# Edge stages of a graph kernel: a hand-fixed order, group by group, in place of the scheduler's

## The chip, the cores and the metric

The kernel runs on one core of a Trainium2 chip. The metric is the device time of one execution in microseconds; beside it stands one profiled execution, whose span and instructions the profile page and the trace show.

## What is computed

Four layers act on x (3125 nodes of 256 numbers), with 53125 edges (src, dst, type, weight). Two of them are graph layers, and the change touches only these:

```python
# heads' graph layer (4 heads of 64), on LayerNorm(x)
feats = einsum('nd,hdo->hno', x, Ws) + bs
score = a_s[:, src] + a_d[:, dst] + aw_e * elem + ab
w = exp(-relu(score / 20))
out = segment_sum(w * feats[:, dst], src) / segment_sum(w, src)
# relations' graph layer (200 relations), on LayerNorm(x)
score = h[src] @ w_src + h[dst] @ w_dst + rel_e @ w_rel
alpha = exp(leaky_relu(score)); alpha = alpha / alpha
agg = segment_sum((h[src] + rel_emb[etype]) @ weight_neighbor * alpha, dst)
node = relu(agg) + where(in_deg > 0, h @ loop_weight, h @ evolve_loop_weight)
```

Each layer's result is added to x. Behind the heads' layer comes a layer of 16 experts with the two best per node, behind the relations' layer a feed-forward layer for half of the nodes ("depths").

## The kernel before

The kernel runs in one program: it sorts the edges by node for the heads (from 0 to about 430 us), computes the table of features, does the heads' edges (430 to 1172), the experts together with the moves of the second sort (to about 1720), the relations' features (to about 1872), the relations' edges (to about 2560) and the depths (to the end).

**Tiles and groups.** The sort has put the edges into tiles of 128, ordered by node tile (128 nodes). There are 25 node tiles, 24 with 18 edge tiles and the last with 8, so 440 edge tiles. `edge_groups` (L714) cuts each node tile into groups of 6, 74 in all; the first of a node tile is called head, the last one last.

**An edge stage.** `edge_stages` (L724) makes three functions, used by the heads' and the relations' edges alike:

- `gather` (L749): at a head, `spread` (L744) loads the row numbers of the whole node tile, broadcast to all partitions (`wide`, 576 KB, two buffers), through SP's queue. Then GpSimd (POOL) issues six indirect gathers (L754) of feature rows into `rows` (three buffers). VectorE (DVE) makes `oh`, the one-hot of each edge's node (L762, three buffers), and `hot`, a one-hot from `wide` (L771): one per group for the heads, three for the relations.
- `message` (L775): TensorE (PE) multiplies `hot` by the nodes' own values into `ps_near` (L780); DVE reduces it (`near`, L787). Then `messages` follows. For the heads (L916) these are three short operations on `s` (L919 to L921), two exponentials on ScalarE (ACT, L924 and L925) and the product `msg` on DVE (L926). For the relations (L1308) they are the weight (L1310 and L1279 to L1282, with an exponential on ACT at L1280), a one-hot of the relation written into the free columns of `rows` (L1313), and six scalings of `oh` to `ohw` on ACT (L1319); `rows` is itself the message.
- `add` (L793): PE sums the messages of a node tile in `ps_sums` (L798). At the last group, SP loads `more` (L804), DVE adds it (`acc`, L806), and `finish` follows. For the heads (L933) it divides, adds to x and calls `done` (L966), which after every five node tiles (and the last two and three) does the next layer norm (`norm_tiles`, L152: statistics, a square root on ACT at L160, scaling), stores its rows, and transposes them and computes the experts' logits on PE. For the relations (L1324) it transposes counts (`ps_cnt`, L1330, copied by ACT at L1333), multiplies them by the relations' features (`ps_rel`, L1336), multiplies the nodes by two loop weights (`ps_loop`, L1343) and adds all to x on DVE (`agg` L1349, `has` L1352 and L1353, `x` L1350 and L1355).

**What sets the order.** `pipelined` (L811) writes step s as gather of group s, message of s-1, add of s-2, and before them one step of `fill`. For the heads, `fill` is the ranking of the second sort, on DVE: after its loads (L224) and one-hots with four matmul steps on PE (L383), 25 steps of five operations over 128 x 416 (such as L441 and L444); for the relations there is none. The Tile framework's scheduler then chooses each engine's order of instructions itself, by readiness and priority; it may run an instruction of a later step ahead of one of an earlier step. Engines wait for each other by semaphores, and a buffer of a pool is handed out again when its last reader is done.

Of the kernel before, what the change touches and what calls it, by code (L numbers as in the profile page):

```python
# [9 lines left out]
F32 = mybir.dt.float32  # L10
BF16 = mybir.dt.bfloat16
# [3 lines left out]
OP = mybir.AluOpType  # L15
# [3 lines left out]
P = 128  # L19
# [3 lines left out]
class _Kernel:  # L23
# [697 lines left out]
                out.append((b, self.first[b] + j, m, j == 0, j + m == n))  # L721
        return out

    def edge_stages(self, pool, st, table, width, into, near, others, messages, W, sums, finish):  # L724

        nc, G = self.nc, self.GRP
        nv = near.shape[3]  # L730
        now = {}


        hold, sums2 = self.ps_a("ps_hold"), self.ps_a("ps_sums")
        numbers = hold[:, :256]
        nc.vector.tensor_copy(numbers, self.iota[:, :256])
        self.numbers, self.weights_ps = numbers, hold[:, 512:]

        def spread(i, b):

            t = pool.tile([P, self.tiles[0] // 2, 2 * P + 8], BF16, name=f"wide{i}")
            src = st["wide"][i][self.first[b] : self.first[b] + self.tiles[b], :]
            src = src.rearrange("(o k i) p -> o k (i p)", o=1, i=2)
            nc.sync.dma_start(  # L744
                t[:, : self.tiles[b] // 2, : 2 * P], src.to_broadcast([P, self.tiles[b] // 2, 2 * P])
            )
            return t

        def gather(g, b, k, n, head, last):  # L749
            if head:  # L750
                now[b] = [spread(i, b) for i in range(len(st["wide"]))]
            rows = pool.tile([P, G, into], F32, name="rows", bufs=3)
            for j in range(n):
                nc.gpsimd.indirect_dma_start(  # L754
                    out=rows[:, j, :width], out_offset=None, in_=table,
                    in_offset=bass.IndirectOffsetOnAxis(
                        ap=st["idx"][:, k + j : k + j + 1], axis=0
                    ),
                )
            sh = [P, n, P]  # L760
            oh = pool.tile([P, G, P], F32, name="oh", bufs=3)
            nc.vector.tensor_tensor(  # L762
                oh[:, :n, :], numbers[:, None, :P].to_broadcast(sh),
                st["row"][:, k : k + n, None].to_broadcast(sh), op=OP.is_equal,
            )
            lo = (k - self.first[b]) // 2
            hots = []
            for i, (at, _) in enumerate([(self.pcol1, None)] + others):
                w = now[b][min(i, 1)][:, lo : lo + n // 2, : 2 * P]
                t = pool.tile([P, G // 2, 2 * P], BF16, name=f"hot{i}", bufs=2)  # L770
                nc.vector.tensor_scalar(t[:, : n // 2, :], w, at, None, op0=OP.is_equal)  # L771
                hots.append(t)
            return rows, oh, hots

        def message(g, b, k, n, head, last, rows, oh, hots):  # L775
            pe = self.ps_b("ps_near")
            picks = [near[:, b]] + [v for _, v in others]
            for j in range(n):
                for i, (t, v) in enumerate(zip(hots, picks)):
                    nc.tensor.matmul(  # L780
                        pe[:, j * 3 * nv : (j + 1) * 3 * nv],
                        t[:, j // 2, j % 2 * P : (j % 2 + 1) * P],
                        v.rearrange("p q v -> p (q v)"),
                        start=(i == 0), stop=(i == len(picks) - 1),
                    )
            own = pool.tile([P, G, nv], F32, name="near")
            nc.vector.tensor_reduce(  # L787
                own[:, :n, :],
                pe[:, : n * 3 * nv].rearrange("p (j q v) -> p j v q", q=3, v=nv), AX.X, OP.add,
            )  # L790
            return messages(k, n, rows, own, oh)

        def add(g, b, k, n, head, last, oh, msg):  # L793
            if head:
                now["sum"] = sums2[:, b % 2 * 512 : (b % 2 + 1) * 512]
            ps = now["sum"]
            for j in range(n):
                nc.tensor.matmul(  # L798
                    ps[:, :W], oh[:, j, :], msg[:, j, :],
                    start=(head and j == 0), stop=(last and j == n - 1),  # L800
                )
            if last:
                more = pool.tile([P, W], F32, name="more")
                nc.sync.dma_start(more, sums[b])  # L804
                acc = pool.tile([P, W], F32, name="acc")
                nc.vector.tensor_add(acc, ps[:, :W], more)  # L806
                finish(b, acc)

        return gather, message, add

    def pipelined(self, stages, fill=()):  # L811


        groups, done = self.edge_groups(), {}
        fill = iter(fill)
        for step in range(len(groups) + len(stages) - 1):
            if step > 2:
                next(fill, None)
            for i, stage in enumerate(stages):
                g = step - i  # L820
                if 0 <= g < len(groups):
                    done[g] = stage(g, *groups[g], *(done.pop(g, None) or ()))
        for _ in fill:
            pass

# [53 lines left out]
    def heads_edges(self, st, fill, done):  # L881
# [26 lines left out]
        with self.tc.tile_pool(name="edge0", bufs=2) as pool:  # L908
            near = pool.tile([P, NT, 3, H], BF16, name="near0p", bufs=1)
            tmp = pool.tile([P, NT, H], F32, name="near0t", bufs=1)  # L910
            self.parts([near[:, :, q, :] for q in range(3)], self.near0[:, :NT, :], tmp)

            own = pool.tile([P, MT, H], F32, name="own", bufs=1)
            own_part(own, st["val"], lambda t, h: t[:, :, h])

            def messages(k, n, rows, near, oh):  # L916
                s = pool.tile([P, G, H], F32, name="s0")
                s = s[:, :n, :]
                nc.vector.tensor_add(s, near[:, :n, :], rows[:, :n, HO:])  # L919
                nc.vector.tensor_add(s, s, own[:, k : k + n, :])  # L920
                nc.vector.tensor_scalar(s, s, -1.0 / 20.0, 0.0, op0=OP.mult, op1=OP.min)  # L921
                msg = pool.tile([P, G, W], F32, name="msg0", bufs=3)
                w = self.weights_ps[:, : n * H].rearrange("p (j h) -> p j h", h=H)
                nc.scalar.activation(w, s, AF.Exp)  # L924
                nc.scalar.activation(msg[:, :n, HO:], s, AF.Exp)  # L925
                nc.vector.tensor_tensor(  # L926
                    msg[:, :n, :HO].rearrange("p j (h o) -> p j h o", o=O),
                    rows[:, :n, :HO].rearrange("p j (h o) -> p j h o", o=O),
                    w[:, :, :, None].to_broadcast([P, n, H, O]), op=OP.mult,
                )  # L930
                return oh, msg

            def finish(b, acc):  # L933
                if b == NT - 1:
                    nc.vector.tensor_scalar(acc[:, HO:], acc[:, HO:], self.norow, None, op0=OP.add)
                r = pool.tile([P, H], F32, name="r0")
                nc.vector.reciprocal(r, acc[:, HO:])
                v = acc[:, :HO].rearrange("p (h o) -> p h o", o=O)
                nc.vector.tensor_tensor(v, v, r[:, :, None].to_broadcast([P, H, O]), op=OP.mult)
                nc.vector.tensor_add(self.x[:, b, :], self.x[:, b, :], acc[:, :HO])  # L940
                done(b)

            self.pipelined(self.edge_stages(
                pool, st, self.table0, W, W, near, [], messages, W, self.sums0, finish
            ), fill)

# [323 lines left out]
    def relations_edges(self, st):  # L1272
# [27 lines left out]
        with self.tc.tile_pool(name="edge1", bufs=2) as pool:  # L1300
# [4 lines left out]
            for i, w in enumerate(("L1_gnn_loop_weight", "L1_gnn_evolve_loop_weight")):  # L1305
                nc.sync.dma_start(lw[:, :, i, :], a[w].rearrange("(c p) d -> p c d", p=P))

            def messages(k, n, rows, near, oh):  # L1308
                s = pool.tile([P, 3, G], F32, name="s1")
                nc.vector.tensor_add(s[:, 0, :n], near[:, :n, 0], rows[:, :n, D])  # L1310
                weight(s[:, 1, :n], s[:, 0, :n], s[:, 2, :n])
                sh = [P, n, R]
                nc.vector.tensor_tensor(  # L1313
                    rows[:, :n, R0:], self.numbers[:, None, :R].to_broadcast(sh),
                    st["val"][:, k : k + n, None].to_broadcast(sh), op=OP.is_equal,
                )
                ow = pool.tile([P, G, P], F32, name="ohw", bufs=3)
                for j in range(n):
                    nc.scalar.activation(  # L1319
# [4 lines left out]
            def finish(t, acc):  # L1324
# [33 lines left out]
                    )  # L1358

            others = [(self.pcols[:, 1 + i : 2 + i], self.rel_p[:, i]) for i in range(-(-R // P))]  # L1360
            self.pipelined(self.edge_stages(
                pool, st, self.table1, R0, W, near, others, messages, W, self.sums1, finish
            ))

# [191 lines left out]
```

## Time and profile before

| what | value |
|---|---|
| median of 3 runs | 2857.28 us (2856.35 to 2861.86) |
| the profiled execution, its own time | 2845.15 us |
| its span | 2842.8 us |
| mean granted clock of PE | 0.822 of full |
| first and last gather of an edge stage (L754) | 429.7 and 2544.1 us |
| gathers: times, median of one | 880, 946 ns |

The span is what the profile's instructions cover; the profiled execution's own time lies 2.35 us over it, and the median of the runs 12 us over that. An instruction group gives its busy time, the mean of one, and how long its engine was idle just before, with the releaser: what that idle time ended on. "remote" is a semaphore event for which the profile has no instruction that ended then. The chain of waits follows the work that ended last back from releaser to releaser; "another core or an unknown queue" is the same unknown there.

### The profile page before, as it was taken

The numbers are of one execution on the slowest core, as the hardware profiler recorded it, in microseconds if no ns is written. First come the engines' busy times: TensorE is split into PE (matmuls) and PEld (weight loads), VectorE is DVE, ScalarE is ACT, GpSimd is POOL, SyncE is SP. The second block draws the span as 40 slices with busy tenths as digits, with TensorE's granted clock in tenths as the row PEclk, the third lists the DMA queues.
The fourth block names the chain that finished last, engine by engine and source line by source line (L and its number), as shares of the span: only waits on it lengthen the run. The fifth ranks groups of instructions, "written<-read, shape, count | busy, mean of one in ns | idle before, by whom it ended". The sixth has DMA issues, their size and how long they took to land.

```text
span 2842.8 us, 24381 instructions
## 1 busy us (share of the span) xinstructions
PE 1878.6 (66%) x7534; PEld 1126.4 (40%) x7534; DVE 1446.3 (51%) x3397; ACT 390.7 (14%) x1097; POOL 1167.4 (41%) x1198
## 2 busy tenths in 40 slices
PE   3169554854544443399999991447878778785298
PEld 0024232543433332356666660323434334343166
DVE  4876225476665343644422224445655556549721
ACT  0000010010000000100112120112222222221012
POOL 4235306576654646034411115036666666650000
PEclk9999996676666667577799996768889888898599
DMA  2000325343444433144499982254545455431000
GB/s 83 0 3 5 104 89 137 93 130 112 115 100 114 116 100 101 49 150 130 131 316 318 317 291 84 87 156 131 148 129 148 130 142 149 128 85 34 8 21 18
DMA packets 258938, 334.04 MB, mean 118 GB/s; under 512 B 30861, under 2 KB 192407, under 8 KB 258807
## 3 DMA queue, kind: packets, MB, share of 16 engines
q1 hardware_dynamic: 197527, 191.26, 21.3%
q0 software_dynamic: 51920, 132.68, 17.6%
q10 hardware_dynamic: 9360, 8.52, 0.9%
q8 instruction: 61, 1.00, 0.1%
q14 instruction: 70, 0.57, 0.1%
HBM read 298.38 MB, written 33.98 MB: 117 GB/s over the span
## 4 chain that ended last, share of the span: by engine, by line
PE 39%; DVE 14%; issue 10%; POOL 9%; another core or an unknown queue 8%; DMA 4%; ACT 1%; SPq 0%; DVEq 0%; POOLq 0%; ACTq 0%
PE ps_sums L798 10%; PE ps_h L1130 9%; POOL rows L754 9%; PE ps_y L1147 4%; PE s_mv L560 3%; DVE cmp L1426 3%; PE ps_hid L1453 3%; PE ps_out L1464 3%; DMA rows<-table,s_idx 3%; DVE msg L926 2%; DVE hot L771 2%; PE ps_x_t L173 1%; PE ps_h_t L173 1%; PE ps_f L1264 1%
## 5 line engine op out<-in xcount | busy, mean ns | idle before, releaser
L754 POOL DMA_INDIRECT rows<-table,s_idx x880 | 848.6, 964 | 725.0 <-issue 240.4
L798 PE MATMUL ps_sums<-msg,oh 128*128 128x260 f32 x880 | 306.6, 519 | 261.8 <-DVE msg L926 143.1
L798 PE MATMUL ps_sums<-rows,ohw 128*128 128x457 f32 x880 | 414.0, 616 | 62.8 <-ACT ohw L1319 54.1
L798 PEld LDWEIGHTS ps_sums<-msg,oh 128*128 128x128 f32 x880 | 226.6, 265 | 325.1 <-issue 250.1
L560 PE MATMUL s_mv<-s_hv,s_hp 128*128 128x200 f16 (+1 forms) x832 | 246.8, 472 | 89.9 <-DVE s_hv L555 89.9
L798 PEld LDWEIGHTS ps_sums<-rows,ohw 128*128 128x128 f32 x880 | 179.0, 215 | 217.5 <-issue 149.6
L1130 PE MATMUL ps_h<-w,x_t 128*128 128x512 f32 x520 | 256.1, 638 | 0.0
L771 DVE TENSOR_SCALAR hot<-wide,pcols 128x768 bf16<-128x768 bf16 (+1 forms) x296 | 175.4, 597 | 73.9 <-PE ps_near L780 63.0
L560 PEld LDWEIGHTS <-s_hp 128*128 128x128 f16 x832 | 122.1, 147 | 208.7 <-issue 180.3
L762 DVE TENSOR_TENSOR oh<-ps_hold,s_row 128x768 f32<-128x768 f32 (+1 forms) x148 | 139.9, 946 | 125.7 <-remote 73.5
L1119 POOL DMA_INDIRECT xg<-xtab,who x65 | 61.9, 952 | 345.1 <-PE ps_x_t L173 302.6
L569 POOL DMA_INDIRECT s_tab<-s_rec,s_to x130 | 147.8, 1137 | 115.1 <-ACT s_rec L566 78.9
L780 PEld LDWEIGHTS <-hot 128*128 128x128 bf16 x1760 | 70.0, 98 | 212.3 <-issue 149.2
L1136 DVE TENSOR_TENSOR hid<-hid,ps_h 128x512 f32<-128x512 f32 x65 | 44.7, 688 | 210.3 <-ACT hid L1135 204.4
L1319 ACT ACTIVATE ohw<-oh,s 128x128 f32<-128x128 f32 x440 | 136.5, 388 | 106.6 <-DVE s L1282 75.2
L1130 PEld LDWEIGHTS ps_h<-w,x_t 128*128 128x128 f32 x520 | 102.8, 209 | 105.7 <-issue 105.5
L926 DVE TENSOR_TENSOR msg<-rows,ps_hold 128x1536 f32<-128x1536 f32 x74 | 128.1, 1731 | 2.0 <-ACT ps_hold L924 1.9
L787 DVE TENSOR_REDUCE near<-ps_near 128x24 f32<-128x72 f32 (+2 forms) x148 | 29.4, 198 | 190.3 <-remote 150.2
L1147 PE MATMUL ps_y<-w,h_t 128*128 128x256 f32 x520 | 122.9, 379 | 0.7 <-ACT h_t L175 0.7
L1147 PEld LDWEIGHTS ps_y<-w,h_t 128*128 128x128 f32 x520 | 98.7, 190 | 41.7 <-issue 30.6
L545 DVE TENSOR_TENSOR s_hp<-num_p,s_pp 128x1024 f16<-128x1024 f16 x104 | 71.8, 690 | 82.8 <-PE s_mv L560 81.4
L1313 DVE TENSOR_TENSOR rows<-ps_hold,s_val 128x1200 f32<-128x1200 f32 x74 | 101.1, 1367 | 6.1 <-PE ps_sums L798 6.1
(307 smaller groups left out, 2344.2 us busy)
## 6 DMA issues: line engine op xcount, KB each, us to landing
w<-in_L_ffn_w_dram SPq DMA_DIRECT2D x195, 512.0 KB
wide<-s_w SPq DMA_DIRECT2D x72, 576.0 KB
rows<-table,s_idx POOLq DMA_INDIRECT x880
ytab<-y ACTq DMA_DIRECT2D x65, 128.0 KB
sums<-sums_z SPq DMA_DIRECT2D x5, 1142.5 KB
more<-sums SPq DMA_DIRECT2D x25, 228.5 KB
sums<-sums_z SPq DMA_DIRECT2D x5, 650.0 KB
table<-f SPq DMA_DIRECT2D x5, 650.0 KB
```

Source lines behind the costliest of these rows:

```text
L560: nc.tensor.matmul(ps[:, : NK * V], hp[:, :, j], rec[:, :, :, j].rearrange("p k v -> p (k v)"), start=(j0 + j == 0), stop=(j0 + j == C - 1),)
L569: d = nc.gpsimd.indirect_dma_start(out=tab, out_offset=bass.IndirectOffsetOnAxis(ap=to[:, i : i + 1], axis=0), in_=out[:, k * CH * V : (k ...
L754: nc.gpsimd.indirect_dma_start(out=rows[:, j, :width], out_offset=None, in_=table, in_offset=bass.IndirectOffsetOnAxis(ap=st["idx"][:, k + ...
L762: nc.vector.tensor_tensor(oh[:, :n, :], numbers[:, None, :P].to_broadcast(sh), st["row"][:, k : k + n, None].to_broadcast(sh), op=OP.is_equal,
L771: nc.vector.tensor_scalar(t[:, : n // 2, :], w, at, None, op0=OP.is_equal)
L798: nc.tensor.matmul(ps[:, :W], oh[:, j, :], msg[:, j, :], start=(head and j == 0), stop=(last and j == n - 1),)
L926: nc.vector.tensor_tensor(msg[:, :n, :HO].rearrange("p j (h o) -> p j h o", o=O), rows[:, :n, :HO].rearrange("p j (h o) -> p j h o", o=O), ...
L1130: nc.tensor.matmul(ph[:, i * HID : (i + 1) * HID], xt[:, c, :], w12[:, i, c, :], start=(c == 0), stop=(c == C - 1),)
L1147: nc.tensor.matmul(py[:, :D], ht[:, c, :], w3[:, c, :], start=(c == 0), stop=(c == HC - 1))
L1313: nc.vector.tensor_tensor(rows[:, :n, R0:], self.numbers[:, None, :R].to_broadcast(sh), st["val"][:, k : k + n, None].to_broadcast(sh), op ...
L1319: nc.scalar.activation(ow[:, j, :], oh[:, j, :], AF.Copy, scale=s[:, 1, j : j + 1])
L1426: nc.vector.tensor_scalar(cmp[:, s:e], wrow[:, s:e], w, None, op0=op, op1=OP.add, accum_out=rank[:, t, i : i + 1],)
```

## The change

`edge_stages` and `pipelined` are replaced by one function, `edges`, whose body stands in `tc.manual_schedule()`: each engine issues the region's instructions in the order in which the program writes them. It writes step g as: the wide loads of group g+2, the gathers of g, its one-hots and `ps_near` matmuls, `prepare` (relations only), message and sums of g-1, the reduce of g, one step of `fill`, and the closing (`acc` and `finish`) of a node tile whose last group was g-2.

- `wide` is loaded per group (half of six times 256 numbers per partition, 192 KB) in four buffers, in place of per node tile in two. `more` is loaded with the wide rows of a head group, before `acc` needs it by a node tile.
- `hot` is made ahead of `oh`, and the `ps_near` matmuls follow them in the same step.
- The relation's one-hot into `rows` (L1313) moves out of `messages` into `prepare`, which runs a step earlier.
- The reduce (`picked`) comes after the message and sums of the group before; `near` has three buffers.
- Gathers, one-hots, matmuls, messages and sums keep their number, shapes and types.

```diff
+        def spread(g):
+            b, k, n = groups[g][:3]
+            wide[g] = []
+            for i, w in enumerate(st["wide"]):
+                t = pool.tile([P, G // 2, 2 * P + 8], BF16, name=f"wide{i}", bufs=4)
+                src = w[k : k + n, :].rearrange("(o k i) p -> o k (i p)", o=1, i=2)
+                nc.sync.dma_start(t[:, : n // 2, : 2 * P], src.to_broadcast([P, n // 2, 2 * P]))
+                wide[g].append(t[:, : n // 2, : 2 * P])
+            if groups[g][3]:
+                more[b] = pool.tile([P, W], F32, name="more")
+                nc.sync.dma_start(more[b], sums[b])
...
+        def message(g):
+            b, k, n, head, last = groups[g]
+            rows, oh, own = live.pop(g)
+            oh, msg = messages(k, n, rows, own, oh)
+            ps = sums2[:, b % 2 * 512 : (b % 2 + 1) * 512]
             for j in range(n):
                 nc.tensor.matmul(
                     ps[:, :W], oh[:, j, :], msg[:, j, :],
                     start=(head and j == 0), stop=(last and j == n - 1),
                 )
+
+        def close(g):
+            b, last = groups[g][0], groups[g][4]
             if last:
...
                 finish(b, acc)
...
+        with tc.manual_schedule():
+            spread(0)
+            spread(1)
+            for g in range(len(groups) + 2):
+                if g + 2 < len(groups):
+                    spread(g + 2)
+                if g < len(groups):
+                    rows = gather(g)
+                    oh, pe = hots(g)
+                    if prepare:
+                        prepare(*groups[g][1:3], rows)
+                if 0 <= g - 1 < len(groups):
+                    message(g - 1)
+                if g < len(groups):
+                    live[g] = rows, oh, picked(g, pe)
+                    if g > 0:
+                        next(fill, None)
+                if 0 <= g - 2:
+                    close(g - 2)
+            for _ in fill:
+                pass
...
+            def prepare(k, n, rows):
+                sh = [P, n, R]
+                nc.vector.tensor_tensor(
+                    rows[:, :n, R0:], self.numbers[:, None, :R].to_broadcast(sh),
+                    st["val"][:, k : k + n, None].to_broadcast(sh), op=OP.is_equal,
+                )
```

More of the change, by code (lines that the diff above doesn't have):

```diff
@@ L722, in edge_groups, with edges @@
         return out
-    def edge_stages(self, pool, st, table, width, into, near, others, messages, W, sums, finish):
-        nc, G = self.nc, self.GRP
+    def edges(
+        self, pool, st, table, width, into, near, others, messages, W, sums, finish,
+        fill=(), prepare=None,
+    ):
+        nc, tc, G = self.nc, self.tc, self.GRP
         nv = near.shape[3]
-        now = {}
         hold, sums2 = self.ps_a("ps_hold"), self.ps_a("ps_sums")
@@ L737, in edge_stages, with gather @@
         self.numbers, self.weights_ps = numbers, hold[:, 512:]
[L739 to L751, printed above, removed]
+        groups = self.edge_groups()
+        wide, live, more, fill = {}, {}, {}, iter(fill)
+        def spread(g):
[9 more added lines that the diff above has]
+                nc.sync.dma_start(more[b], sums[b])
+        def gather(g):
+            k, n = groups[g][1:3]
             rows = pool.tile([P, G, into], F32, name="rows", bufs=3)
@@ L759, in gather, with hots @@
                 )
+            return rows
+        def hots(g):
+            b, k, n = groups[g][:3]
             sh = [P, n, P]
+            made = []
+            for i, (at, _) in enumerate([(self.pcol1, None)] + others):
+                t = pool.tile([P, G // 2, 2 * P], BF16, name=f"hot{i}", bufs=2)
+                nc.vector.tensor_scalar(
+                    t[:, : n // 2, :], wide[g][min(i, 1)], at, None, op0=OP.is_equal
+                )
+                made.append(t)
             oh = pool.tile([P, G, P], F32, name="oh", bufs=3)
@@ L765, in gather @@
             )
[L766 to L775, printed above, removed]
             pe = self.ps_b("ps_near")
@@ L778, in message @@
             for j in range(n):
-                for i, (t, v) in enumerate(zip(hots, picks)):
+                for i, (t, v) in enumerate(zip(made, picks)):
                     nc.tensor.matmul(
@@ L785, in message, with picked @@
                     )
-            own = pool.tile([P, G, nv], F32, name="near")
+            return oh, pe
+        def picked(g, pe):
+            n = groups[g][2]
+            own = pool.tile([P, G, nv], F32, name="near", bufs=3)
             nc.vector.tensor_reduce(
@@ L790, in message @@
             )
[L791 to L796, printed above, removed]
+            return own
+        def message(g):
[3 more added lines that the diff above has]
+            ps = sums2[:, b % 2 * 512 : (b % 2 + 1) * 512]
             for j in range(n):
@@ L801, in add @@
                 )
+        def close(g):
+            b, last = groups[g][0], groups[g][4]
             if last:
-                more = pool.tile([P, W], F32, name="more")
-                nc.sync.dma_start(more, sums[b])
                 acc = pool.tile([P, W], F32, name="acc")
-                nc.vector.tensor_add(acc, ps[:, :W], more)
+                nc.vector.tensor_add(
+                    acc, sums2[:, b % 2 * 512 : b % 2 * 512 + W], more.pop(b)
+                )
                 finish(b, acc)
[L809 to L824, printed above, removed]
+        with tc.manual_schedule():
[19 more added lines that the diff above has]
+                pass
     def heads_features(self):
@@ L941, in finish @@
                 done(b)
-            self.pipelined(self.edge_stages(
-                pool, st, self.table0, W, W, near, [], messages, W, self.sums0, finish
-            ), fill)
+            self.edges(
+                pool, st, self.table0, W, W, near, [], messages, W, self.sums0, finish, fill
+            )
     def gate(self, pool):
@@ L1306, in relations_edges @@
                 nc.sync.dma_start(lw[:, :, i, :], a[w].rearrange("(c p) d -> p c d", p=P))
[L1308 to L1311, printed above, removed]
+            def prepare(k, n, rows):
                 sh = [P, n, R]
@@ L1316, in messages @@
                 )
+            def messages(k, n, rows, near, oh):
+                s = pool.tile([P, 3, G], F32, name="s1")
+                nc.vector.tensor_add(s[:, 0, :n], near[:, :n, 0], rows[:, :n, D])
+                weight(s[:, 1, :n], s[:, 0, :n], s[:, 2, :n])
                 ow = pool.tile([P, G, P], F32, name="ohw", bufs=3)
@@ L1360, in relations_edges @@
             others = [(self.pcols[:, 1 + i : 2 + i], self.rel_p[:, i]) for i in range(-(-R // P))]
-            self.pipelined(self.edge_stages(
-                pool, st, self.table1, R0, W, near, others, messages, W, self.sums1, finish
-            ))
+            self.edges(
+                pool, st, self.table1, R0, W, near, others, messages, W, self.sums1, finish,
+                prepare=prepare,
+            )
     def depths(self):
```

## The prediction

> **What bounds the kernel now.** I read the page first (busy time, groups), then the busy time by stretch, the waits, and the chain and timeline in two places where it stops. No engine is full over the whole span:
>
> ```profile
> span 2842.8 us, 24381 instructions
> ...
> PE 1878.6 (66%) x7534; PEld 1126.4 (40%) x7534; DVE 1446.3 (51%) x3397; ACT 390.7 (14%) x1097; POOL 1167.4 (41%) x1198
> ```
>
> so the two edge stages must be read alone. The busy time by stretch (columns: us, then PE, weight loads, DVE, ACT, POOL with instructions, clock, DMA share, GB/s), first the heads' edges, then the relations' edges:
>
> ```profile
> 430.00:1172.00 742.00, 384.19 (x1586) 282.81 (x1586) 412.05 (x973) 51.81 (x191) 433.13 (x442) 0.68 0.40 108
> ...
> 1872.00:2560.00 688.00, 527.82 (x2491) 266.88 (x2492) 379.45 (x958) 172.23 (x588) 415.01 (x439) 0.86 0.50 136
> ```
>
> The page's group of the gathers shows why POOL is the floor though it is busy only 60% there:
>
> ```profile
> L754 POOL DMA_INDIRECT rows<-table,s_idx x880 | 848.6, 964 | 725.0 <-issue 240.4
> ```
>
> Each gather is about 0.95 us and has 0.30 us of issue behind it (240.4 us over 789 times): 1.25 us, 7.5 us for a group of 6, 22.5 us for a node tile of 18, 440 x 1.25 = 550 us per stage. In the heads' stage the mean gather is 433/440 = 0.98 us, so its floor is 433 + 132 = 565 us. It runs from 429.7 to about 1158, 728 us: 163 us over the floor. The relations' gathers settle at 27.3 us per node tile (2106.7, 2134.0, 2161.3 and so on in the raw starts): 4.8 us over, about 115 us in the stage. The waits say what POOL lacks; a gather needs the buffer of rows from three groups before:
>
> ```profile
> POOL rows L754 <- DVE msg L926: 161.5, 19, 23.6
> ...
> DVE near L787 <- remote: 150.2, 30, 12.3
> ...
> DVE oh L762 <- remote: 73.5, 9, 14.0
> DVE acc L806 <- remote: 70.8, 6, 18.4
> POOL rows L754 <- PE ps_sums L798: 73.8, 25, 14.3
> ```
>
> (total, times, longest.) The three "remote" waits are DVE waiting for a semaphore of PE: 294.5 us, about the 163 + 115 us lost. One of them in the chain of waits of the heads' stage, where POOL runs dry because `msg` has not freed `rows`:
>
> ```profile
> 1080.92 1.75 DVE msg L926
> 1082.67 14.01 another core or an unknown queue
> 1096.68 0.02 issue
> 1096.71 0.04 DVE oh L762
> ```
>
> The timeline has PE's last recorded matmul there (sums, from 1082.82, 4.37 us) over by 1087.2. The same in the relations' stage, small and once per node tile:
>
> ```profile
> 2123.09 0.18 DVE L787 TENSOR_REDUCE near<-ps_near 128x6 f32<-128x18 f32 x1 [4.54 <-remote]
> ...
> 2123.50 0.94 POOL L754 DMA_INDIRECT rows<-table,s_idx  x1 [2.80 <-PE ps_near L780]
> ```
>
> **What the skill says.** The Trainium skill, "Perfetto Trace Analysis", Tensor Engine Instruction: a matmul's end is computed from its size, not observed. That fits: DVE waits up to some 10 us past PE's recorded end, so I can't say from the trace what PE still does. The same section calls DVE and ACT strictly FIFO, while only weight loads move ahead on PE; so a wait written into the fixed order holds all behind it. "TensorE: Matmul & The Clock Gate", Part 1: half clock after an idle window of about 3.4 us. The trace agrees: a sums batch of the heads takes 2.87 us, and 5.5 at half clock; one of the relations 4.7 and 7.0 (2098.73). "DMA: Bandwidth & Descriptors", Anatomy of one DMA: about 2 us fixed to completion; here rows land 2.2 us after a gather's end on POOL.
>
> **The change, part by part.**
>
> *Order in the heads' stage.* Same arithmetic, same gathers. Per group DVE has hot 0.60, oh 0.95, three s operations 0.52, msg 1.74, reduce 0.22, and about 0.3 for ACT's exp that msg waits for: 4.3 us; a step of the ranking adds 0.37 + 0.2 + 1.0 + 0.58 + 0.58 = 2.7 for some 41 groups; closing a tile 1.4/3 = 0.5. That is 7.5 us beside POOL's 7.7 (565/74), so DVE just keeps up while the ranking runs, and later at 4.8 easily. Now msg(g-1) stands ahead of the reduce and of the next near; it no longer waits for a near that PE reports late. It can end about 5 us after its gather ended on POOL; the buffer is wanted 15 us after, so some 10 us of lateness are free. Most stalls of 4 to 14 us should shrink or go. What stays: `done(b)` for five tiles. DVE stands in order behind statistics 3.0, a square root on ACT with its table load 1.28 + 0.3, scaling 1.7, and transposes and logits of about 6.5: 13 us, then hots 1.55 and msg 2.8. Worked from a group's start on POOL: DVE is free at +9.5, through with `done` at +22.5, with the next message at +28, where the gather three on is due at +22.5. That is 3 to 6 us while the ranking leaves no slack to catch up (twice), about 3 after it (three times): 21 us. The ranking's first steps wait for their loads, and four of them have 32 matmuls (9 us on PE); I put 10 us for both. The floor 565 + 21 + 10 is 596 against 728: 132 gained at full effect. I don't know what keeps PE's report late, so part of it may stay; bounds 0 (the lateness is all within the slack) and 80 (half of the loss): I take 30. **Heads: -100**, bounds -160 and -50.
>
> *Order in the relations' stage.* Here `rows` is freed by the sums on PE, not by msg. A gather that starts at 0 has landed at 9.7; s chain with ACT's exp 1.1, ohw's first tile 0.45, sums 4.7: about 16, wanted at 22.5. Free is 6 us at most. Once per node tile, though, close(g-2) stands on DVE ahead of the next hots, and its agg and x need, on PE behind sums(g-1), cnt 0.6, rel, x_t 0.4, loop 1.9 with ACT's copies between: about 5.8 us to the last x. So DVE's round is: three times hots 1.8 + 0.95, prepare 1.37, s chain 1.05 and reduce, less what overlaps, 5.1 each = 15.3; then 0.45 + 4.7 for the last sums; then 5.8: 26.3 us, without overlap 28.1. Before it is 27.3. The new order thus takes the late near off the path of the message and puts the late close on it. I take 26.5: 25 x -0.8 = **-20 us**. Bounds: -110 (23 us per tile, if close hides), +50 (sums at half clock in this round, 29.3).
>
> *prepare moved* ahead of the message, 1.37 us per group on DVE: it fills time in which DVE waits for rows anyway, but if close is late it stands ahead of the message, 25 x 1.37 = 34 us; that is inside the 15.3.
>
> *Wide rows per group.* 75 SP issues become 222, with the same bytes: 0.4 us of SP each, 147 x 0.4 = 59 us on an engine that is nearly idle and, with four buffers, issued two groups (15 us) ahead: 0, where a load that came late would hold hots, and through the slack its group, by some 3 us. Queued behind such a wait on SP are `more`, the store of normed rows and the ranking's loads, due within two groups: up to +5 each for the few loads, so 0 to +10, and I take 0. At the head of the relations' stage the chain shows 8.07 us for the first two 576 KB loads; two of 192 KB should be about 3: **-5**. `more` two groups earlier, `near` with a third buffer: 0, never late on the chain. The fixed order itself adds no instruction.
>
> *What lay between.* In the relations' stage DVE also does 24 of the 25 statistics of the next layer norm (L157 and L158, 0.42 + 0.18 us each), emitted after the stage. If they stay between, 0; if all come after it, 24 x 0.6 = +14; I take **+5**.
>
> Sum: -100 - 20 - 5 + 5 = -120. The profiled execution took 2845.15 us (span 2842.8 and 2.35 around it): 2725. The median of the runs, 2857.28, is 12 us above that execution: **2737 us**.
>
> **Rivals.** A, the forecast: heads mostly freed, relations about equal, 2680 to 2790; chance 0.46. B, both stages come near to the gather floor, since near off the path is all that mattered: -150 - 100 - 5 gives 2602; for it speaks that "remote" waits cover the whole loss, against it that close's 5.8 us stands in DVE's order; 0.22. C, PE's late report follows wherever DVE next waits for PE (acc, the logits, the reduce): heads -45, relations 0: 2810; for it, oh and acc wait "remote" as well as near; 0.18. D, slower: relations' close with PE at half clock, as PE idles about 6 us in each round between loop and the next sums: sums +2.3 and close's PE part +3 on 26.3, 31.6 us per tile, +4.3 x 25 = +107, with the heads at only -50: 2914. It decides from 31.3 us per tile at a full gain of the heads, from 29.3 at half; against it, PE's mean clock is 0.86 here and PE has 20 us of work in 28; 0.10. E, the scheduler's order was already this one: 2857; the stalls with near ahead of msg speak against it; 0.04.
>
> **Numbers.** Faster by over 0.2% (about what a measurement of this kernel can tell from no change): A, B and C, less a little of C, 0.85; within: 0.05; slower: D, 0.10. The range takes A, most of B and most of C: 2600 to 2825.
>
> **What would show it.** Right: gathers in 610 to 650 us in the heads' stage; the waits of POOL on msg under 60 us; stalls left only at `done`; relations at 26 to 27 us per tile with DVE's x or agg waiting for PE loop and rel. Wrong: "remote" waits of 150 us or more, or a relations' period of 22.5 to 24 (B) or 29 and more (D); hot waiting for wide loads.

## The result, and the profile after

| kernel | median (runs) | ratio to before, 95% interval |
|---|---|---|
| before, measured beside it | 2859.57 us (2856.35 to 2891.97, 4) | |
| after | 3234.53 us (3229.91 to 3238.63, 4) | 1.128 [1.120, 1.137] |

The change makes the kernel 13% slower; forecast was 2737 us. The profile of after has a span of 3236.9 us. By the starts and ends of the gathers in the trace, the heads' edges take 837 us from the first gather to the last one's end (728 before), the relations' edges 948 (674 before): +109 and +274 of the 394 us between the two profiled executions (375 between the medians). What lies outside the two stages grew by 11 us in all.

The groups and the waits of after (columns as before):

```profile
span 3236.9 us, 24598 instructions
...
L763 POOL DMA_INDIRECT rows<-table,s_idx x880 | 843.0, 958 | 1113.9 <-PE ps_sums L813 350.0
...
L801 DVE TENSOR_REDUCE near<-ps_near 128x24 f32<-128x72 f32 (+2 forms) x148 | 29.7, 201 | 436.3 <-remote 301.4
...
L822 DVE TENSOR_TENSOR acc<-ps_sums,more 128x260 f32<-128x260 f32 (+1 forms) x50 | 26.6, 531 | 233.0 <-remote 209.7
```

```profile
DVE near L801 <- remote: 301.4, 38, 15.4
...
PE ps_near L790 <- DVE hot L777: 243.6, 98, 16.0
...
DVE acc L822 <- remote: 209.7, 38, 12.5
```

The gathers are as fast as before (958 ns), but POOL is idle 389 us longer. The waits named remote did not shrink from 294.5 us; those of near and acc alone are 511 us. And PE now waits 244 us for `hot`, where before it had waited 57.5. One round of the heads, once the ranking is over, shows how these belong together (timeline: start, duration, engine, idle before):

```profile
1060.42 2.87 PE L813 MATMUL ps_sums<-msg,oh 128*128 128x260 f32 x12 [1.40 <-DVE msg L949]
...
1067.47 0.23 DVE L801 TENSOR_REDUCE near<-ps_near 128x24 f32<-128x72 f32 x1 [7.19 <-remote]
...
1075.99 0.43 DVE L822 TENSOR_TENSOR acc<-ps_sums,more 128x260 f32<-128x260 f32 x1 [8.28 <-remote]
...
1077.46 0.61 DVE L777 TENSOR_SCALAR hot<-wide,pcols 128x768 bf16<-128x768 bf16 x1
...
1078.13 0.33 PE L790 MATMUL ps_near<-near0p,hot 128*128 128x12 bf16 x6 [14.84 <-DVE hot L777]
...
1081.80 0.95 POOL L763 DMA_INDIRECT rows<-table,s_idx  x1 [9.10 <-DVE near L801]
```

DVE takes its instructions in the written order; I call this order its line. It waits 7.2 us for near and at once 8.3 us for acc. The next `hot` stands behind both, so PE has nothing to do for 14.8 us. POOL stands still for 9.1 us, since the message that frees its buffer comes later still in DVE's line (the trace names near, the instruction right behind that message). By the records PE was done with these sums at 1063.3. By PE's semaphore events in the trace the sums before it were done at 1062.49, near at 1067.45, these sums at 1075.96: 8.51 us for twelve matmuls, 0.71 us each, where the records have 0.24. The ends in the records are modelled, so the trace does not tell whether PE worked late or only reported late. "Late" means below that PE's semaphore event comes well after the recorded end.

**Chips differ.** The experiments ran on five chips. On three of them the kernel before took 2634 to 2647 us and PE's events follow the recorded ends by 0.01 to 0.02 us; on the other two it took 2847 and 2920 us, with remote waits as in the profiles of the prediction and the result. I call these chips in time and late. Each was used at one time only, so the runs do not tell a property of the chip from a condition that comes and goes; which chip the result ran on is not on record. Times and ratios below are only set against the kernel before on the same chip.

### The profile page after: what moved, and what is told of

Same layout as the page of the kernel before. It is cut to its first block, busy times and chain, and to the rows that moved or that the text cites. A ratio compares the mean times of both kernels' runs of the same rounds, so it can differ in the third digit from the quotient of the medians.

```text
span 3236.9 us, 24598 instructions
## 1 busy us (share of the span) xinstructions
PE 1976.1 (61%) x7534; PEld 1165.9 (36%) x7534; DVE 1509.5 (47%) x3397; ACT 393.4 (12%) x1097; POOL 1162.1 (36%) x1198
## 3 DMA queue, kind: packets, MB, share of 16 engines
q8 instruction: 62, 1.02, 0.1%
## 5 line engine op out<-in xcount | busy, mean ns | idle before, releaser
L813 PE MATMUL ps_sums<-msg,oh 128*128 128x260 f32 x880 | 313.4, 526 | 174.1 <-DVE msg L949 84.2
L777 DVE TENSOR_SCALAR hot<-wide,pcols 128x768 bf16<-128x768 bf16 (+1 forms) x296 | 165.0, 599 | 6.4 <-issue 6.4
L790 PE MATMUL ps_near<-near0p,hot 128*128 128x12 bf16 x440 | 23.2, 172 | 206.8 <-DVE hot L777 190.5
L822 DVE TENSOR_TENSOR acc<-ps_sums,more 128x260 f32<-128x260 f32 (+1 forms) x50 | 26.6, 531 | 233.0 <-remote 209.7
L1355 PE MATMUL ps_cnt<-ident,acc 128*128 128x128 f32 (+1 forms) x50 | 22.1, 441 | 180.1 <-DVE acc L822 171.2
```

Source lines behind the costliest of these rows:

```text
L777: nc.vector.tensor_scalar(t[:, : n // 2, :], wide[g][min(i, 1)], at, None, op0=OP.is_equal)
L790: nc.tensor.matmul(pe[:, j * 3 * nv : (j + 1) * 3 * nv], t[:, j // 2, j % 2 * P : (j % 2 + 1) * P], v.rearrange("p q v -> p (q v)"), start ...
L813: nc.tensor.matmul(ps[:, :W], oh[:, j, :], msg[:, j, :], start=(head and j == 0), stop=(last and j == n - 1),)
```

## The experiments

| kernel | chip | median us | before there | ratio | heads, us | relations, us |
|---|---|---|---|---|---|---|
| before, again | in time | 2637 (1 run) | 2636 | | 589 | 617 |
| after, again | in time | 2822 | 2636 | 1.071 [1.065, 1.077] | 645 | 731 |
| wide per node tile | in time | 2822 | 2634 | 1.070 [1.064, 1.077] | 655 | 723 |
| scheduler's order | in time | 2610 | 2634 | 0.990 [0.988, 0.992] | 582 | 602 |
| acc early | in time | 2806 | 2634 | 1.064 [1.058, 1.070] | 621 | 738 |
| old steps, fixed | in time | 2662 | 2636 | 1.009 [1.006, 1.012] | 632 | 596 |
| closing split | in time | 2628 | 2636 | 0.997 [0.995, 0.998] | 623 | 564 |
| tail later | in time | 2666 | 2647 | 1.007 [1.005, 1.009] | 637 | 583 |
| ranking behind | in time | 2919 | 2647 | 1.103 [1.100, 1.106] | 581 | 733 |
| heads free, relations split | in time | 2581 | 2647 | 0.976 [0.974, 0.978] | 583 | 557 |
| the same | late | 3007 | 2920 | 1.030 [1.023, 1.037] | 730 | 821 |
| after, third time | late | 3221 (1 run) | 2847 | 1.13 | 823 | 943 |

Heads and relations are the times from a stage's first gather to its last gather's end in the trace.

**Which part of the change.** First the order and the wide loads apart, the move of acc, and the gathers taken away.

The order left to the scheduler:

```diff
-        with tc.manual_schedule():
+        with ExitStack():
```

> The changed kernel, with its order of writing, but without the fixed-order region: the scheduler orders each engine again. If the fixed order is what costs: 2800 to 2920 us. If what is written (near in the step of its one-hots, prepare early, wide per group, more early) costs: 3100 or more.

Measured 2609.82 us, ratio 0.990. The band was drawn for a late chip; as a ratio to 2860 it is 0.98 to 1.02, and the run lies in it. On a chip in time all that the change writes, without the fixed order, is a gain of 1%; the fixed order turns it into a loss of 7%. On a late chip this version was not run.

The wide rows per node tile again, in the fixed order:

```diff
-                t = pool.tile([P, G // 2, 2 * P + 8], BF16, name=f"wide{i}", bufs=4)
+                    t = pool.tile([P, self.tiles[0] // 2, 2 * P + 8], BF16, name=f"wide{i}")
...
+            wide[g] = [t[:, lo : lo + n // 2, : 2 * P] for t in whole[b]]
```

> The changed kernel with wide loaded per node tile in two buffers again, two groups ahead of the head. Theories A and B: 3234 plus or minus 25 us. Rival C (147 more loads on SP and small transfers beside the gathers): 3000 us or less.

Measured 2822 us where after itself takes 2822 on such a chip: the number and size of the loads cost nothing in the sum (the heads 10 us more, the relations 8 less). (The band of the expectation was drawn for the late chip; it is the ratio that answers.)

acc ahead of the message:

```diff
+                if 0 <= g - 2:
+                    add_up(g - 2)
                 if 0 <= g - 1 < len(groups):
                     message(g - 1)
```

> The changed kernel with one step moved: acc (the sum of a finished node tile) stands ahead of message(g-1) in place of behind it; finish stays where it was. Theory A (the fixed order makes DVE wait, in order, for work on PE that reports late; acc waits for the sums of the NEXT group, 8 us per tile of the heads and 3.5 of the relations, and the next group's one-hots stand behind it): those waits go, 2990 to 3100 us. Rival B (the closing chain cnt, rel, loop at half clock is the cost): at most 30 us faster than 3234. Rival C (the wide loads per group): no change.

Ratio 1.064 in place of 1.071. Acc's wait fell from 178 us (after on a chip in time) to 55 and the heads gained 23 us. In the relations the wait only moved to the closing's next instruction: agg waited 193 us for PE's rel in place of 53, since PE does the closing behind the same sums. Theory A is right for the heads and too simple for the relations.

Plain loads for the gathers, in after:

```diff
-                nc.gpsimd.indirect_dma_start(
...
+                at = (k + j) % self.NT * P
+                nc.sync.dma_start(rows[:, j, :width], table[at : at + P, :])
```

> The changed kernel with the indirect gathers on POOL replaced by plain loads of 128 consecutive rows on SP's queue, same bytes into the same places (it leaves out the choice of rows by edge). If PE's late reports come with the gathers on POOL: no DVE wait named remote over 20 us in all, stages at DVE's and PE's own pace, about 2450 to 2650 us. If they come from PE, its clock or the order itself: the remote waits stay over 300 us and the time over 3000.

Inconclusive: 2866.64 us, ratio 1.087, on a chip in time, where no kernel shows remote waits, with gathers or without. The row loads now stand in SP's queue behind `more`, and SP waits there for DVE to free a buffer, 739 us in all; what this costs was not worked out.

**The same two kernels on a chip in time.**

> The kernel before, unchanged, for a trace on the chip of the experiments, where it took 2634 us and not 2857. Theory A (the waits named remote come with late reports of PE that one chip shows and another doesn't): no remote wait over 20 us in all, heads' gathers in about 610 us, relations' node tile in 24 to 26 us. If the two chips differ in something else: the remote waits are there again.

Before: 2637 us, no remote waits, heads 589 and relations 617 us (25.2 per node tile; the expectation said 24 to 26, and 610 for the heads). So of the 163 and 115 us over the gather floors of 565 and 550 us that the prediction wanted to win, a chip in time has 24 and 67.

> The changed kernel, unchanged, for its ratio and trace on the chip of the experiments. By the run with wide loads per node tile: 2822 us plus or minus 15, ratio 1.06 to 1.08, acc waiting for PE's sums some 180 us, no remote waits. If the late reports come back: 3200 and ratio 1.13.

After: 2822 us, ratio 1.071 [1.065, 1.077], no remote waits. One node tile of the relations, DVE and two of PE's batches of sums, is the working of the prediction's 26.5 us with measured numbers:

```profile
2100.01 1.64 DVE L777 TENSOR_SCALAR hot<-wide,pcols 128x768 bf16<-128x768 bf16 x3
...
2105.51 6.26 PE L813 MATMUL ps_sums<-rows,ohw 128*128 128x457 f32 x12 [3.22 <-ACT ohw L1344]
...
2112.25 0.18 DVE L801 TENSOR_REDUCE near<-ps_near 128x6 f32<-128x18 f32 x1 [2.40 <-PE ps_near L790]
...
2117.39 0.18 DVE L801 TENSOR_REDUCE near<-ps_near 128x6 f32<-128x18 f32 x1 [0.17 <-PE ps_near L790]
...
2117.72 4.87 PE L813 MATMUL ps_sums<-rows,ohw 128*128 128x457 f32 x12 [0.36 <-ACT ohw L1344]
...
2122.63 0.64 DVE L822 TENSOR_TENSOR acc<-ps_sums,more 128x457 f32<-128x457 f32 x1 [5.06 <-PE ps_sums L813]
...
2125.39 0.42 DVE L1374 TENSOR_TENSOR agg<-acc,ps_rel 128x256 f32<-128x256 f32 x1 [2.13 <-PE ps_rel L1361]
```

From the first hot to the third reduce it takes 17.6 us. Of these 2.4 are a wait for near, which PE does behind the sums of two groups before; those took 6.26 us in place of 4.87, as PE's granted clock was 0.50 from 2101.6 to 2108.3. Then come 5.1 us for acc and 6.4 to the last x (agg comes 2.8 after acc's start, and in the tile before the last x ended 3.7 after agg's start): 29.1; over the stage 731/24.4 = 29.9 us. Acc waits until PE's sums of the next group end (4.87 us from 2117.72), though it reads the half of the bank pair that was finished a group ago; why it is held for the other half was not tested. POOL, whose buffers are freed by sums, stood still earlier in the same tile, where those sums came late:

```profile
2112.05 0.94 POOL L763 DMA_INDIRECT rows<-table,s_idx  x1 [6.71 <-PE ps_sums L813]
```

**Is it the fixed order as such?** The kernel before with its own steps, fixed:

```diff
+        with self.tc.manual_schedule():
+            for step in range(len(groups) + len(stages) - 1):
...
```

> The kernel before, its steps written as they were, but inside the fixed-order region. If fixing an order costs by itself (each engine stands in line behind waits that the scheduler would have passed): 2720 us or more. If only the new place of acc and of the closing chain costs: 2600 to 2680 us, like before.

2662 us, ratio 1.009: inside the second band. The relations get faster (596 against 617), the heads slower (632 against 589). So a fixed order as such is not what costs in the relations. Here too the closing stands on DVE ahead of the next one-hots, but PE sums each group one step later, so that the closing follows the tile's own sums and not those of the next group. Acc then hardly waits (total us, times, longest; this run, then after on a chip in time):

```profile
DVE agg L1350 <- PE ps_rel L1337: 56.9, 25, 2.9
...
DVE acc L806 <- PE ps_sums L798: 7.8, 4, 3.7
```

```profile
DVE acc L822 <- PE ps_sums L813: 177.8, 46, 5.3
```

The closing in two parts:

```diff
+                if 0 <= g - 3:
+                    close(g - 3)
                 if 0 <= g - 1 < len(groups):
                     message(g - 1)
...
-                if 0 <= g - 2:
-                    close(g - 2)
+                if 0 <= g - 3:
+                    tail(g - 3)
```

> The changed kernel with the closing of a node tile in two parts, still in fixed order: acc and PE's part a step later, behind the next one-hots and ahead of the message; DVE's tail (agg, has, x; for the heads done) behind the reduce. If the cost of the change is that the next one-hots stand on DVE behind acc and the closing chain: relations 23 to 25.5 us per node tile in place of 30, in all 2600 to 2700 us. If it is the fixed order as such: 2780 or more.

2627.68 us, ratio 0.997. The relations run at 564 us, 23.1 per node tile, 14 us over the 550 of the floor: 167 us less than after, for moving the same closing instructions by a step.

The tail alone moved:

```diff
-                if 0 <= g - 2:
+                if 0 <= g - 3:
+                    tail(g - 3)
+                if 0 <= g - 2 < len(groups):
                     close(g - 2)
```

> The changed kernel with one move alone: DVE's tail of the closing (agg, has, x; for the heads done) stands behind the reduce of the next step; acc and PE's part stay where the change put them. If the wait for acc (5 us per tile) and the tail's wait for PE (5.5 us) each stand on DVE's line and add up: relations about 25 us per node tile, 630 us in place of 731, in all about 2710. If acc's wait is what counts: 28 us or more, 2770 or more.

2665.74 us: relations 583 us, 23.9 per node tile, better than the 25 expected. Acc still waits 165 us in all, and the stage is fast all the same; acc moved alone gained nothing there (738). By these two runs it is the sum of both waits on one line that does not fit, not acc's wait by itself. The tail's move takes the relations from 731 to 583, and moving acc and PE's part as well takes them to 564.

The heads gain little that way (623 and 637 against 645). The ranking behind the groups:

```diff
-                    if g > 0:
-                        next(fill, None)
```

> The changed kernel with the ranking of the second sort written behind the heads' groups and not between them. If the heads lose by the ranking's steps in DVE's line: gathers of the heads in 590 us or less in place of 645, and then some 115 to 140 us of ranking alone, in all 2870 to 2910. If they lose by acc and done in line: 620 us or more for the gathers, in all over 2910.

Heads' gathers in 581 us. The five stalls of POOL that stay are at `done`, four of 6.8 to 6.9 us, and one of 3.1 at the end (six in this view with one of 0.3):

```profile
POOL rows L763 <- DVE near L801: 30.9, 6, 6.9
```

So 64 us of the heads' stage are the ranking's steps in DVE's line; as a whole it is slower, 2919 us, since the ranking then stands alone.

The best of both, the heads in the scheduler's order and the relations in the fixed one with the closing split:

```diff
-        with tc.manual_schedule():
...
+        lag = 3 if fixed else 2
+        with tc.manual_schedule() if fixed else ExitStack():
```

> The heads' edges with the changed kernel's writing but the scheduler's order (582 us from the first gather to the last there), the relations' edges in fixed order with the closing split and a step later (564 us). If the stages add up: before less 7 and less 53, 2575 us, ratio 0.975 to 0.98. If a stage's order shifts work into its neighbours: 2600 or more.

2580.83 us, ratio 0.976 [0.974, 0.978], as added up. It beats both kernels, on a chip in time.

> The version of e9 once more, for another chip. Where PE reports in time (before at about 2640 us): ratio 0.97 to 0.98 again. Where PE reports late while gathers run (before at about 2857 us, as in the prediction's profile): the relations' fixed order still has near and acc ahead of other work on DVE, so the waits named remote come back, and the ratio is 0.97 to 1.05.

On a late chip the same kernel loses: 1.030. Its remote waits of near are back (307 us), and of oh (97 us). The heads, in the scheduler's order, take 730 us, about what the kernel before took in the profile of the prediction (728; after 837); the relations, in the fixed order, take 821 (674 there).

**What the late reports come with.**

> The kernel before with plain loads of 128 consecutive rows on SP's queue in place of the gathers on POOL (it leaves out the choice of rows by edge). On a chip where PE reports late: if that comes with the gathers, no remote waits, and the edge stages lose what the order of SP's queue costs alone; if not, remote waits as before. On a chip without late reports: no remote waits either way, and it says nothing on them.

On a late chip: 2396.78 us against 2846.69 (one run each). The largest waits named remote in after on that chip, and then all of them in this kernel:

```profile
DVE acc L822 <- remote: 241.2, 39, 11.7
...
DVE near L801 <- remote: 236.7, 33, 15.5
...
POOL rows L763 <- remote: 57.7, 22, 2.7
```

```profile
DVE ln_mv L158 <- remote: 1.9, 1, 1.9
```

The nearest neighbour with gathers, the next run, has 235 us for oh, near and acc on the same chip. So PE's late reports come with the gathers through POOL; that rests on one run of one late chip, and on the times at which they begin and end (last section). The time as a whole also lacks the gathers' floor, so its 16% is not the price of the late reports.

> The kernel before with the row of numbers that oh and the relations' one-hot read in SBUF in place of PSUM. On a chip where PE reports late: if DVE's reads of PSUM hold PE up, the remote waits fall by half or more and the time by 100 us or more; if not, within 30 us of before. On another chip: within 30 us.

```diff
-        numbers = hold[:, :256]
-        nc.vector.tensor_copy(numbers, self.iota[:, :256])
+        numbers = self.iota[:, :256]
```

2817.21 us against 2846.69, remote waits of oh, near and acc still 235 us, so DVE's reads of these numbers in PSUM are not what makes PE late. Its other reads of PSUM (msg, near, acc) were left as they are and are not ruled out.

> The changed kernel once more beside them: ratio to before 1.07 where PE reports in time, 1.12 to 1.14 with remote waits of 400 us or more where it reports late.

3220.89 us, 1.13, on a late chip: the ratio of the result again.

## Why the prediction was wrong

- **The floor and its distance.** 565 and 550 us for the gathers hold: the scheduler's order comes to 582 in the heads, the split closing to 557 in the relations. What lay above the floor was misread. The remote waits (294.5 us) were taken for about the whole of the 278 us lost, and for a matter of the order. A chip in time has none of them and still 24 and 67 us over the floor; on late chips they are there in every order that was run with gathers.
- **"It no longer waits for a near that PE reports late ... some 10 us of lateness are free" (heads, -100; measured +109, on a chip in time +56).** This step failed, together with the term "closing a tile 1.4/3 = 0.5", which has DVE's busy time and nothing for a wait. The slack was counted for POOL's buffer, as if each wait had it to itself. But near's reduce and acc stand one behind the other on DVE, and the next hot behind them. In the round shown their waits of 7.2 and 8.3 us add up to 15.5, over the 10 that were to be free, and stop PE for 14.8 us and POOL for 9.1. And "DVE just keeps up while the ranking runs" left no slack for any wait: with PE in time, taking the ranking out of the line brought the heads from 645 to 581 us.
- **Closing in the relations (26.5 us per node tile; measured 29.9 in time, 38.8 late).** The place was right, the size was not. The term of three groups was 15.3 and is 17.6, by near's wait of 2.4; the closing was 5.8 and is 6.4 with acc. The 5.15 for the last sums holds (5.06). "Without overlap 28.1" does not come out of the terms given (3 x 5.4 + 5.15 + 5.8 = 27.1), and I chose the low end. The profile of before could not show near's wait in this order, and I did not bound it.
- **The late chip's part** in the relations is 8.9 us per node tile. In the tile shown here near's third reduce waits 8.4 us (0.2 in time) and acc 3.5 (5.1 in time), both "remote" and together 6.7 us more; and loop takes 3.8 us in place of 2.0, at a granted clock of 0.50 (2313 to 2325).

```profile
2308.78 0.18 DVE L801 TENSOR_REDUCE near<-ps_near 128x6 f32<-128x18 f32 x1 [8.42 <-remote]
...
2312.47 0.64 DVE L822 TENSOR_TENSOR acc<-ps_sums,more 128x457 f32<-128x457 f32 x1 [3.52 <-remote]
...
2317.03 3.78 PE L1368 MATMUL ps_loop<-lw,x_t 128*128 128x512 f32 x4 [0.46 <-issue]
```

- **`done`** was worked out as 3 to 6 us while the ranking runs (twice) and about 3 after it, 21 us in all. POOL's stalls there, in after on a chip in time, are 14.4 us twice, then 7.8, 6.8 and 3.1: 46 us. With the ranking out of the way four are 6.8 to 6.9 and the last 3.1. The term came to less than half of what was measured.
- **Wide loads, prepare, statistics**: no cost, as said (2822 us with either way of loading; the statistics still run between, at 0). The start of the relations gained about 1 us and not 5: the first hot comes 6.7 us after the first gather, 7.8 before (in time 7.3 and 7.1); the loads of three groups are issued there one right after the other.
- **The rivals.** D had the right place (closing on DVE's line), the right sign, at 10%, and a mechanism that both profiles show. Its half-clocked sums (+2.3 us) are there in part in time (6.3 us in place of 4.9, some 1.4 of near's 2.4 us by my estimate) and in full late (7.6 us from 2327.3). Its 31.6 us per tile lie between the 29.9 in time and the 38.8 late; it had no late near. C named what the late chip adds ("PE's late report follows wherever DVE next waits for PE"), but as a smaller gain and not as a loss. Neither had both together, and the range ended at 2825.

Of the 375 us, a chip in time shows 186 (2822 less 2636) as the price of the change without late reports; the rest comes where late reports meet it. By which path gathers on POOL hold PE's completions up, and why only on some chips, stays open: no run here shows it.

## What to carry to other kernels

In a fixed order, work out for each in-order engine the round through its waits. Add up every wait that stands on the same line, and do not hold each against its own slack. A closing step that waits for another engine should not come after the next group's work on that engine and before the next group's work on its own. Two orders avoided this: the closing behind the next one-hots and messages (731 us to 564), and the sums a step later, so that the closing follows its own (596).

If the profile's worst waits have no releaser in it, ask first whether they follow the order at all: the kernel before on another chip had none. Both orders pay for late reports, the fixed one more: across the chips, the scheduler's lost 2860 - 2636 = 224 us, the fixed one 3234 - 2822 = 412.

## What the runs showed of the hardware

The Trainium skill, "Perfetto Trace Analysis", Tensor Engine Instruction, says that a matmul's semaphore goes out only once PSUM has acknowledged the write, after the modelled end. On chips in time the two lie 0.01 to 0.02 us apart. On late chips they come apart in the edge stages, some 5 us after a run of gathers starts: by up to 12 us in the relations and more in the heads. The events then follow each other 0.71 us per matmul (twelve of them in the heads' round above). In the kernel before, 25 of the relations' near matmuls, of 3 columns each, also start 0.70 to 0.71 us after the one ahead of them, where 0.03 is usual, with no wait that the trace names. So at least there PE itself was held, and not only its report. The events catch up about when the last gather has landed. In the sort and the experts, with PE busy and gathers on POOL too, no event of the traces from late chips lay more than 0.6 us behind the nearest recorded end before it.
